# Attention on one core: the products with v put together behind the second step of side work, and the long product of a side step put first

## The chip, the core and the metric

The kernel runs on one core of one Trainium2 chip. The metric is the device time of one execution in microseconds (us). Within a core several engines run their own instruction streams, each in order, and wait for one another through semaphores: TensorE (PE in the profile; its weight loads are PEld), VectorE (DVE), ScalarE (ACT), GpSimd (POOL) and the queue that issues most transfers (SP).

## The reference

The reference is one transformer layer on 4 sequences of 512 tokens of width 512, in float32.

```python
x = x + cross_attention(layernorm(x), ctx)     # 16 heads of 32
x = x + moe(layernorm(x)) + shared_swiglu(layernorm(x))
```

In the cross attention, `q` comes from the tokens, `k` and `v` from a context of 512 rows of width 256. Queries and keys are normalized per head. The last 16 context rows have weights, keys and values of their own, and their attention is a second softmax whose result is added to that over the other 496 rows. The output is projected by `Wo`. Then a router picks 6 of 64 experts for each token, each expert takes at most 384 tokens and applies a gated feed-forward of width 352; a shared feed-forward of width 704 is added.

## The kernel before

The work has four stages in time: weights and the first context (up to about 110 us), the attention loop (to about 665 us) with the routing inside it, the shared feed-forward of the first sequences, and then the 64 experts with the combination at the end.

In the attention loop the 2048 tokens are 16 tiles of 128, and a tile is worked in four units, one for each group g of four heads. For a unit, `scores` (L351) multiplies queries and keys into two score tiles `ps`; `maximum` (L357, VectorE) takes row maxima `nm`; `exponentials` (L361, ScalarE) writes the probabilities `pr` and their sums; `mix_tail` (L368 and L369, VectorE) writes the 16 columns of the second softmax beside them. Then `turned` (L376) transposes each of the four slices of 128 keys into a bank `x`, `copied` (L381) copies it to `pT` (three by ScalarE, the fourth by VectorE), and `values` (L387) multiplies it with v into `pc`. The scores of the next unit are issued ahead of the transpositions of this one.

The loop that emits all this is written out by hand, and the order in which it is written is the order of the instructions on TensorE, ScalarE, VectorE and GpSimd. No planner changes it.

Into each unit two steps of side work are put by calls of `beside()`; there are thus eight numbered steps per tile, 0 to 7. Side work is a list of generators, each of which does one piece whenever it is asked:

- "query" (`query_tile`) prepares the queries of the tile after next: layer normalization on VectorE and GpSimd (`xn`, L313, then L314) at step 0, transposition of `xn` (L233) and copy `xnT` (L318) at step 2, the projection `mm` (L264) in two halves at steps 4 and 5, then `head_norm`: centring `hn_cen` (L242), square `hn_sq` (L244, GpSimd), and at step 0 of the next tile the variance (L248), a power on GpSimd (L251) and scaling (L252); at its step 3 the transposition into `qT`, at step 6 the scores of the 16 extra rows (L333 to L340).
- "context" (`context_tile`) prepares 128 rows of k and v for the next sequence: transposition at step 1, the k projection with its centring at step 2, the v projection (L305) with variance, power and scaling at step 3, the transposition of the keys at step 6. The fourth context tile of a sequence begins at step 5 of the tile before, so that its products are at steps 6 and 7. The last sequence has none to prepare, so tiles 12 to 15 run without.
- "finish" (`finish`) ends a tile: at step 7 it scales `pc`, at steps 0 and 1 come the two halves of the output projection with `wo`, the second layer normalization and `h` (L413, GpSimd), and in later tiles the transposition of h (step 4), the router (L433 to L443 at step 2, L456 to L459 at step 4, L462 to L473 at step 5) and six scatters of token numbers by GpSimd (L477, two each at steps 6, 7 and 0).

`owner` (L547) names for each of the eight steps the generator kind whose piece is a long projection there: finish at 0 and 1, context at 2 and 3, query at 4 and 5, none at 6 and 7. `beside()` sorts the list by whether a generator is of that kind; every generator of the kind is moved, also one of another tile that has no product at that step.

Three kinds of PSUM buffer matter: two banks `x`, taken in turn by all transpositions and small products, one bank `mm` for projections, and one bank `pc`. Whoever needs a bank again waits until its reader has emptied it.

Of the kernel before, what the change touches and what calls it, by code (L numbers as in the profile page):

```python
# [15 lines left out]
P = 128  # L16
B, S, D = 4, 512, 512
SC, KD = 512, 256
# [23 lines left out]
def xattn_moe_kernel(ctx, tc, a, out):  # L42
# [63 lines left out]
    def load_shared():  # L106
        for c in range(NC):
            sh_gu.append(slab(2 * FS))
            nc.sync.dma_start(sh_gu[-1], a["sh_guT"][c * P:(c + 1) * P, :])
        for f in range(0, len(FSC), 3):  # L110
            sh_down.append(slab(3, D))
            full = min(3, FS // P - f)
            nc.sync.dma_start(sh_down[-1][:, :full, :],
                              a["sh_downT"][f * P:(f + full) * P, :].rearrange("(c p) n -> p c n", p=P))
            if full < 3:
                nc.sync.dma_start(sh_down[-1][:FS % P, full, :], a["sh_downT"][(f + full) * P:, :])
# [39 lines left out]
    with ExitStack() as att:  # L156
# [188 lines left out]
        def scores(g, qT, kT):  # L345

            pss = []
            for r in range(NC):
                if r % 2 == 0:
                    pss.append(ps_s.tile([P, 2, SC], F32, tag="ps", name="ps"))  # L350
                nc.tensor.matmul(pss[-1][:, r % 2, :SM], qT[r * HD:(r + 1) * HD, g, :],  # L351
                                 kT[r * HD:(r + 1) * HD, g, :SM], start=True, stop=True)
            nm = small.tile([P, NC], F32, tag="nm", name="nm")
            return pss, nm

        def maximum(pss, nm, i):
            nc.vector.tensor_reduce(nm[:, 2 * i:2 * i + 2], pss[i][:, :, :SM], AX.X, ALU.max, negate=True)  # L357

        def exponentials(pr, pss, nm, sm, g, i):
            for r in (2 * i, 2 * i + 1):  # L360
                nc.scalar.activation(pr[:, r, :SM], pss[i][:, r % 2, :SM], AF.Exp, bias=nm[:, r:r + 1],  # L361
                                     accum_out=sm[:, g * NC + r:g * NC + r + 1])

        def mix_tail(pr, g, pd, rd, sm):

            hs = slice(g * NC, (g + 1) * NC)
            f = small.tile([P, NC], F32, tag="f", name="f")
            nc.vector.tensor_tensor(f, sm[:, hs], rd[:, hs], ALU.mult)  # L368
            nc.vector.tensor_tensor(pr[:, :, SM:], pd[:, hs, :], f.unsqueeze(2).to_broadcast([P, NC, DCA]),  # L369
                                    ALU.mult)  # L370
# [8 lines left out]
        def copied(tp, engine):  # L379
            pT = w2.tile([P, NC, P], F32, tag="pT", name="pT", bufs=5)  # L380
            (engine.copy if engine is nc.scalar else engine.tensor_copy)(pT, tp)  # L381
            return pT

        def values(pc, g, c, pT, kv):
            for r in range(NC):
                h = g * NC + r
                nc.tensor.matmul(pc[r * HD:(r + 1) * HD, g, :], kv[:, c, h * HD:(h + 1) * HD], pT[:, r, :],  # L387
                                 start=c == 0, stop=c == SC // P - 1)

        def inverse_sums(sm):  # L390

            rs = small.tile([P, H], F32, tag="rs", name="rs")
            nc.vector.reciprocal(rs, sm)
            wide = w2.tile([P, H, HD], F32, tag="wide", name="wide", bufs=1)
            nc.gpsimd.tensor_copy(wide, rs.unsqueeze(2).to_broadcast([P, H, HD]))
            return wide
# [114 lines left out]
        def new_context():  # L511
            return slab(NC, SC), slab(SC // P, D)
# [4 lines left out]
        def run(gens):  # L517

            left = []
            for g in gens:  # L520
                try:
                    next(g)
                    left.append(g)
                except StopIteration:
                    pass
            return left
# [5 lines left out]
        kvs, qTs, tail = {0: new_context()}, {}, {}  # L532
# [24 lines left out]
        for i in range(0, len(first), 2):  # L557
            side = first[i:i + 2]
            while side:
                side = run(side)  # L560
# [3 lines left out]
        side = []  # L564

        def beside():

            side.extend((n, make()) for n, make in begin.pop(step[0], ()))
            last = owner[step[0] % per_tile]
            for part in sorted(side, key=lambda p: p[0] == last):  # L570
                if next(part[1], side) is side:
                    side.remove(part)
            step[0] += 1

        def load_batch(b):
            for tn in range(b * TB, (b + 1) * TB):
                nc.sync.dma_start(acc[:, tn, :], a["x"][tn * P:(tn + 1) * P, :])
            load_y(b)
# [3 lines left out]
        with tc.manual_schedule(engines=engines):  # L582
            new = scores(0, qTs[0], kvs[0][0])
            pr = w2.tile([P, NC, SC], F32, tag="pr", name="pr")
            for i in range(2):
                maximum(*new, i)
                exponentials(pr, *new, tail[0][2], 0, i)
            for u, (t, g) in enumerate(units):
                b, i = divmod(t, TB)
                pd, rd, sm = tail[t]  # L590
                if g == 0:
                    pc = ps_c.tile([P, NC, P], F32, tag="pc", name="pc")
                    if i == 2 and b + 2 < B:
                        load_batch(b + 2)
                    if t == NT - 2:
                        load_shared()
                mix_tail(pr, g, pd, rd, sm)
                if g == NC - 1:
                    wide = inverse_sums(sm)
                pr_u = pr  # L600
                if u + 1 < len(units):
                    tn, gn = units[u + 1]
                    new = scores(gn, qTs[tn], kvs[tn // TB][0])
                    pr = w2.tile([P, NC, SC], F32, tag="pr", name="pr")
                pT = [copied(turned(pr_u, c), nc.scalar) for c in range(2)]
                if u + 1 < len(units):
                    maximum(*new, 0)
                    maximum(*new, 1)
                    exponentials(pr, *new, tail[tn][2], gn, 0)
                beside()  # L610
                pT.append(copied(turned(pr_u, 2), nc.scalar))
                pT.append(copied(turned(pr_u, 3), nc.vector))
                if u + 1 < len(units):
                    exponentials(pr, *new, tail[tn][2], gn, 1)
                for c in range(2):
                    values(pc, g, c, pT[c], kvs[b][1])
                if g < NC - 1:
                    beside()
                for c in range(2, SC // P):
                    values(pc, g, c, pT[c], kvs[b][1])  # L620
                if g == NC - 1:
                    side.append(("finish", finish(t, pc, wide)))
                    beside()

            class Here:
                hid = staticmethod(lambda: w2.tile([P, NC, SC], F32, tag="pr", name="pr")[:, :3, :])
                sg = staticmethod(lambda: w2.tile([P, NC, P], F32, tag="pT", name="pT", bufs=5).rearrange(
                    "p a b -> p (a b)"))
                pair = staticmethod(lambda: (lambda ps: (ps[:, 0, :], ps[:, 1, :]))(
                    ps_s.tile([P, 2, SC], F32, tag="ps", name="ps")))  # L630
                pd = staticmethod(lambda: ps_s.tile([P, 2, SC], F32, tag="ps", name="ps")[:, 0, :])

            def advance(steps, n):
                for _ in range(n):
                    next(steps, None)

            (_, oldest), (_, older), (_, newer) = side
            advance(oldest, 1)
            work = shared(0, Here)
            next(work)  # L640

            for n_older, n_newer in ((5, 2), (4, 0), (0, 3), (0, 2), (0, 4), (0, 2)):
                next(work)
                advance(older, n_older)
                advance(newer, n_newer)
                next(work)
            advance(newer, 4)
            lists_made = plan()
            for _ in range(TB):
                next(lists_made, None)  # L650
                next(work)
            for steps in (oldest, older, newer, lists_made, work):
                assert next(steps, None) is None
# [180 lines left out]
    with tc.manual_schedule(engines=engines):  # L834
# [64 lines left out]
        for i, b in enumerate(late):  # L899
            for n, _ in enumerate(others[b]):  # L900
# [8 lines left out]
                last = step == len(late) * slices  # L909
# [53 lines left out]
```

## Time and profile before

| | us |
|---|---|
| median of three runs | 1899.08 (1897.15 to 1904.79) |
| the profiled execution | 1896.93 |
| its span, from first to last instruction | 1895.1 |
| TensorE busy in the span | 1738.1 (92%) |
| VectorE, ScalarE, GpSimd busy | 852.3, 601.4, 677.7 |
| mean granted TensorE clock | 0.972 |

The profile is of one execution. Its lines name the engine, the line of the kernel, the operation, what it writes and reads by the program's names, and in brackets how long the engine stood idle before it and which instruction released it. A float32 product appears as two TensorE records. Times in the timeline are microseconds from the start of the span. The shares of busy time are means over stages with different limits, so a change inside the attention loop has to be read from that stretch. The granted clock is the share of full speed that TensorE was allowed.

### The profile page before, as it was taken

The page shows a single profiled execution, that of the slowest core. Times are in us where ns is not written, and L with a number is a line of the kernel's source. Part 1 is how long each engine was busy: PE and PEld are TensorE (multiplying, and loading weights), DVE is VectorE, ACT ScalarE, POOL GpSimd, SP SyncE. Part 2 cuts the span into 40 slices and gives each one's busy share as a digit, 9 for nine tenths or more (in the row PEclk, how much of TensorE's full clock was granted, in tenths as well). Part 3 has the DMA queues.
Part 4 walks back from the last instruction along what each step waited for, and adds up shares of the span by engine and source line. Part 5 has one row for each costly group of instructions (what it writes and reads, how often), then busy time and mean ns, then how long its engine had stood idle before and what let it go on. Part 6 is the DMA issues. An engine that isn't in the chain of part 4 may idle for free.

```text
span 1895.1 us, 28083 instructions
## 1 busy us (share of the span) xinstructions
PE 1738.1 (92%) x10556; PEld 1134.2 (60%) x10556; DVE 852.3 (45%) x1656; ACT 601.4 (32%) x1326; POOL 677.7 (36%) x620
## 2 busy tenths in 40 slices
PE   4689998999899898999999999999999999999994
PEld 1255555555555543476767767777777777666441
DVE  4256777777777732132322333333333333222565
ACT  0155565556566620022222222222232222222000
POOL 5435666655755332021211111221212122110776
PEclk9789999999999999999999999999999999999997
DMA  7000000010110114166876777787888787755676
GB/s 252 2 7 20 21 16 18 18 33 12 43 55 26 46 34 142 40 225 229 264 231 233 254 241 268 255 275 269 277 283 288 263 270 266 232 198 161 185 229 207
DMA packets 122658, 302.62 MB, mean 160 GB/s; under 512 B 16560, under 2 KB 44496, under 8 KB 114224
## 3 DMA queue, kind: packets, MB, share of 16 engines
q1 hardware_dynamic: 94928, 220.76, 34.2%
q0 software_dynamic: 26400, 76.16, 13.2%
q8 instruction: 197, 3.23, 0.7%
q10 hardware_dynamic: 1088, 2.10, 0.3%
q14 instruction: 45, 0.37, 0.1%
HBM read 235.28 MB, written 63.55 MB: 158 GB/s over the span
## 4 chain that ended last, share of the span: by engine, by line
PE 74%; DVE 10%; POOL 9%; DMA 3%; issue 3%; ACT 2%; SPq 0%; POOLq 0%; DVEq 0%
PE pg L743 16%; PE pd L782 10%; PE pu L743 10%; PE pd L788 6%; PE mm L264 5%; DVE nm L357 4%; PE x L376 3%; PE tx L731 3%; PE pu L764 3%; PE pg L128 3%; POOL hn_r L251 3%; PE pu L128 3%; PE pc L387 2%; PE pd L145 2%; PE x L233 2%
## 5 line engine op out<-in xcount | busy, mean ns | idle before, releaser
L690 POOL DMA_INDIRECT xg<-h_d,lists x192 | 182.0, 948 | 790.5 <-PE tx L731 716.1
L743 PE MATMUL pg<-xT,wgu 128*128 128x192 f32 (+4 forms) x1536 | 320.2, 351 | 11.2 <-issue 10.8
L743 PEld LDWEIGHTS pg<-xT,wgu 128*128 128x128 f32 x1536 | 257.8, 190 | 77.9 <-issue 57.9
L755 DVE TENSOR_TENSOR ehid<-sg,pu 128x384 f32<-128x384 f32 x128 | 70.9, 554 | 452.1 <-PE pu L743 446.7
L782 PE MATMUL pd<-wd,ehid 128*128 128x512 f32 (+1 forms) x408 | 213.2, 609 | 0.7 <-ACT eo L811 0.7
L743 PE MATMUL pu<-xT,wgu 128*128 128x192 f32 (+4 forms) x1024 | 205.9, 344 | 0.0
L754 ACT ACTIVATE sg<-pg 128x384 f32<-128x384 f32 x128 | 62.9, 491 | 380.2 <-PE pg L743 380.2
L743 PEld LDWEIGHTS pu<-xT,wgu 128*128 128x128 f32 x1024 | 176.0, 191 | 12.2 <-issue 1.5
L361 ACT ACTIVATE pr<-ps,nm 128x496 f32<-128x496 f32 x256 | 171.0, 677 | 17.3 <-DVE nm L357 16.4
L376 PEld LDWEIGHTS x<-ident,pr 128*128 128x128 f32 x1024 | 116.4, 145 | 92.7 <-issue 60.0
L381 ACT COPY pT<-x 128x512 f32<-128x512 f32 x192 | 106.6, 586 | 194.6 <-PE x L376 192.7
L376 PE MATMUL x<-ident,pr 128*128 128x128 f32 x1024 | 147.1, 286 | 14.8 <-DVE r_hot L458 8.3
L357 DVE TENSOR_REDUCE nm<-ps 128x2 f32<-128x992 f32 x128 | 145.2, 1173 | 17.2 <-PE ps L351 17.1
L788 PE MATMUL pd<-wd,ehid 128*64 128x256 f32 x1092 | 131.3, 384 | 9.0 <-ACT uh L771 4.4
L251 POOL TENSOR_TENSOR hn_r<-hn_var,mhalf 128x16 f32<-128x16 f32 (+1 forms) x33 | 96.6, 2927 | 95.6 <-DVE hn_var L249 80.7
L733 DVE COPY xT<-tx 128x512 f32<-128x512 f32 x192 | 126.0, 685 | 3.6 <-PE tx L731 2.1
L477 POOL DMA_INDIRECT list_d<-token_id,r_put x96 | 100.5, 1047 | 27.4 <-issue 24.9
L769 DVE TENSOR_TENSOR ehid<-sg,pg 32x384 f32<-32x384 f32 x64 | 35.8, 559 | 162.4 <-ACT sg L768 162.4
L788 PEld LDWEIGHTS pd<-wd,ehid 128*64 128x64 f32 x1092 | 78.1, 138 | 48.1 <-issue 7.4
L387 PE MATMUL pc<-pT,slab 128*32 128x128 f32 x2048 | 86.1, 289 | 3.4 <-DVE pT L381 2.7
L387 PEld LDWEIGHTS pc<-pT,slab 128*32 128x32 f32 x2048 | 50.5, 113 | 50.9 <-issue 39.9
L873 POOL DMA_INDIRECT g<-eo_d,slot_get x48 | 51.9, 1081 | 78.1 <-issue 66.7
(161 smaller groups left out, 2363.6 us busy)
## 6 DMA issues: line engine op xcount, KB each, us to landing
wgu<-in_w_gu SPq DMA_DIRECT2D x64, 1408.0 KB, 6.9
wd<-in_w_down SPq DMA_DIRECT2D x64, 512.0 KB, 6.6
eo_d<-eo SPq DMA_DIRECT2D x64, 512.0 KB, 5.2
eo_d<-eo SPq DMA_DIRECT2D x128, 128.0 KB, 4.8
wd<-in_w_down SPq DMA_DIRECT2D x64, 192.0 KB, 6.7
acc<-in_x SPq DMA_DIRECT2D x16, 256.0 KB, 5.2
h_d<-h SPq DMA_DIRECT2D x16, 256.0 KB, 2.0
h2T_d<-hT SPq DMA_DIRECT2D x16, 256.0 KB, 2.3
```

The source lines that it names most:

```text
L128: nc.tensor.matmul(dst, sh_gu[c][:, w0:w0 + P], xT[:, c, :], start=c == 0, stop=c == NC - 1)
L251: nc.gpsimd.tensor_tensor(r[:m], var[:m], mhalf[:m], ALU.pow)
L357: nc.vector.tensor_reduce(nm[:, 2 * i:2 * i + 2], pss[i][:, :, :SM], AX.X, ALU.max, negate=True)
L361: nc.scalar.activation(pr[:, r, :SM], pss[i][:, r % 2, :SM], AF.Exp, bias=nm[:, r:r + 1], accum_out=sm[:, g * NC + r:g * NC + r + 1])
L376: nc.tensor.transpose(tp[:, r, :], pr[:, r, c * P:(c + 1) * P], ident)
L381: (engine.copy if engine is nc.scalar else engine.tensor_copy)(pT, tp)
L387: nc.tensor.matmul(pc[r * HD:(r + 1) * HD, g, :], kv[:, c, h * HD:(h + 1) * HD], pT[:, r, :], start=c == 0, stop=c == SC // P - 1)
L690: nc.gpsimd.indirect_dma_start(out=x[:, :], out_offset=None, in_=h2_d[:, :], in_offset=bass.IndirectOffsetOnAxis(ap=lists[:, e * CT + c:e ...
L733: nc.vector.tensor_copy(xT[:, :, c * P:(c + 1) * P], tp)
L743: nc.tensor.matmul(dst[:, :n], wgu[:, c, w0:w0 + P], xT[:, c, :n], start=c == 0, stop=c == NC - 1)
L782: nc.tensor.matmul(pd, hid[:fn, fc, m * P:(m + 1) * P], wd[:fn, fc, :], start=fc == 0, stop=fc == len(FC) - 1)
L788: nc.tensor.matmul(pd[d * HALF:(d + 1) * HALF, i * D // 2:(i + 1) * D // 2], hid[:fn, fc, P + i * HALF:P + (i + 1) * HALF], wd[:fn, fc, d ...
```

## The change

Two edits in the attention loop. The key of the sort in `beside()` is inverted, so that at steps 0 to 5 the generators of the owner's kind come first and not last. And the products of the first two key slices with v no longer stand ahead of the second call of `beside()` of a unit: all four slices follow it. In the last unit of a tile, where the second call stands at the end, the order of the products stays as it was.

```diff
             side.extend((n, make()) for n, make in begin.pop(step[0], ()))
             last = owner[step[0] % per_tile]
-            for part in sorted(side, key=lambda p: p[0] == last):
+            for part in sorted(side, key=lambda p: p[0] != last):
                 if next(part[1], side) is side:
                     side.remove(part)
             step[0] += 1
...
                 if u + 1 < len(units):
                     exponentials(pr, *new, tail[tn][2], gn, 1)
-                for c in range(2):
-                    values(pc, g, c, pT[c], kvs[b][1])
                 if g < NC - 1:
                     beside()
-                for c in range(2, SC // P):
+                for c in range(SC // P):
                     values(pc, g, c, pT[c], kvs[b][1])
                 if g == NC - 1:
                     side.append(("finish", finish(t, pc, wide)))
```

Counted over the whole program, each engine has the same instructions as before. On TensorE, 16 v products follow one another where two groups of 8 had side work between them; on VectorE, the centring `hn_cen` (L242) now precedes the routing operations L433 to L443 at step 2 and L462 to L473 at step 5; on GpSimd, the two scatters of step 0 now precede the power, the scaling and `xn` of that step; on ScalarE, the key scaling (L258) precedes the copy `xnT` in three tiles; the order of SP's transfers is the same.

## The prediction

> **What bounds the kernel now.** I read the page first. TensorE is busy for 92% of the span, and the slices show where it is not full.
>
> ```profile
> PE 1738.1 (92%) x10556; PEld 1134.2 (60%) x10556; DVE 852.3 (45%) x1656; ACT 601.4 (32%) x1326; POOL 677.7 (36%) x620
> ```
>
> The change is confined to the attention loop (about 110 to 665 us). A table of stretches gives that stage's load; the columns are stretch, length, then busy us (and instructions) of PE, weight load, DVE, ACT, POOL, then clock, DMA share and GB/s.
>
> ```profile
> 150.00:650.00 500.00, 455.91 (x3986) 273.62 (x3988) 366.76 (x811) 294.88 (x729) 298.19 (x241) 0.98 0.08 26
> ```
>
> TensorE is full 91% of the time and the next engine, VectorE, 73%; DMA is 8%. At most 44 us of 500 are TensorE gaps, and only those can be won. The waits of TensorE from 109 to 612 us (total, times, longest) name them:
>
> ```profile
> PE x L233 <- POOL xn L313: 23.4, 13, 2.3
> PE x L376 <- DVE r_hot L458: 5.7, 6, 1.0
> PE x L233 <- DVE r_nm L426: 2.3, 8, 0.3
> ```
>
> The timeline of query tile 6 (its first scores start at 317.43) shows how each arises: start, length, engine, instruction, and in brackets the idle time before.
>
> ```profile
> 322.26 2.94 POOL L251 TENSOR_TENSOR hn_r<-hn_var,mhalf 128x16 f32<-128x16 f32 x1 [6.00 <-DVE hn_var L249]
> 326.95 2.08 POOL L313 TENSOR_SCALAR xn<-acc,ln_mv,ln_r 128x512 f32<-128x512 f32 x1
> 329.08 0.66 PE L233 MATMUL x<-ident,xn 128*128 128x128 f32 x4 [1.61 <-POOL xn L313]
> 329.57 1.88 PE L264 MATMUL mm<-slab,yT 128*128 128x512 f32 x4
> 341.38 0.53 DVE L458 TENSOR_TENSOR r_hot<-r_hot,x 128x384 f32<-128x384 f32 x1
> 341.97 1.09 PE L376 MATMUL x<-ident,pr 128*128 128x128 f32 x8 [0.95 <-DVE r_hot L458]
> 345.76 0.69 DVE L242 TENSOR_TENSOR hn_cen<-mm,bq 128x512 f32<-128x512 f32 x1 [0.32 <-PE mm L264]
> 346.53 1.04 POOL L244 TENSOR_TENSOR hn_sq<-hn_cen 128x512 f32<-128x512 f32 x1 [4.15 <-DVE f L368]
> 346.56 1.10 DVE L369 TENSOR_TENSOR pr<-pd,f 128x64 f32<-128x64 f32 x1
> 347.74 2.21 DVE L357 TENSOR_REDUCE nm<-ps 128x2 f32<-128x992 f32 x2
> 350.89 0.63 PE L233 MATMUL x<-ident,hn_sq 128*128 128x128 f32 x4 [0.28 <-DVE r_nm L426]
> ```
>
> To be seen: at step 2 of a tile TensorE waits 1.6 us for POOL's normalized rows and has a ready 1.88 us product right behind; at step 4 it waits 0.95 us for VectorE's L458; at step 6 it is released by VectorE, with no slack.
>
> [...]L369 takes 0.23 us alone, 1.10 us beside L244 (above). [...]after the 2.34 us waits of tiles 3 and 7 the granted clock read 0.50 in 222 to 224 and 372 to 374 us, after that of tile 11 it read 1.00; the 1.6 us waits left it at 1.00.
>
> **The change, part by part.** No instruction is added or removed. I count from tile 6's first scores (t = 0); tile numbers from 0.
>
> *Products with v (16 records, 0.64 us) move behind the second side step.* TensorE's sum is unchanged. What is lost is a cover: where the second side step starts with a transposition into an x bank and not with a product, that now follows the probabilities' transpositions at once and waits for ACT to empty a bank (copy 0.59, less the other 0.5 us of transpositions, plus hand-over: 0.3). This is step 3 of tiles 0, 3, 7, 11, 12, 13 and 14: 7 x 0.3 = **2 us lost**. The wait for the third and fourth pT copy does not grow: everything before it on TensorE stays.
>
> *Step 2, product first* (tiles 1, 2, 4, 5, 6, 8, 9, 10: those with a context product there). Before: free at 10.0, xn ready at 11.65. After: the product fills 10.0 to 11.9, then the xn transposition runs at once. But the product no longer covers xnT's copy: the transposition ends 12.5, ACT copies 12.6 to 13.2, and the second following transposition needs that bank; its predecessor ends 13.0, so some 0.4 to 0.45 us is paid back. 1.6 - 0.45 = 1.15; x 8 = **9.2 us won**. The product's VectorE reader hn_cen goes ahead of the routing work (max, index, hot, goes: 2.7 us), whose queue holds pT's fourth copy; that copy ends near 15.8, needed at 17.2, so hidden by the next product and v products; uncovered it would cost what it is late.
>
> *Step 4* (4, 5, 6, 8, 9, 10). The query product first removes the 0.24 us wait of L456 on pT, and in step 3 VectorE is earlier, since POOL's square no longer stands behind two scatters. L458 then comes 0.1 us after its bank's matmuls, 0.54 long, with 0.5 us of h transpositions as cover: 0.2 to 0.25 us of waiting stays. 0.95 + 0.24 - 0.25 = 0.94; I take 0.8, because hn_cen's place makes VectorE's line less free: 6 x 0.8 = **4.8 us won**.
>
> *Step 5, VectorE's queue* (tiles 2 to 13). Before, the eight routing operations L462 to L473 (1.6 us) ran while the product ran; after, hn_cen waits for the product's end E, and they follow it. hn_cen ends E + 0.75, L462 (0.54) E + 1.25, POOL's square runs E + 0.85 to 1.9; L464 [...]is held to 1.9; L464 to L473 take 1.06, f, the tail product and the reciprocal 0.45: the row maximum nm starts at E + 3.4. Before it started at E + 2.0 (347.74 - 345.72, the product's 343.84 + 1.88). The scores now follow at E + 1.15, as all 1.28 us of v products lie between, before at E + 0.5. So nm is 0.7 to 0.8 us later against TensorE, and step 6 has no slack: TensorE's transposition waits on VectorE (0.28 before). 12 x 0.8 = **9.6 us lost**. If L464 slips in before the square, 0.2; I take 0.8, since L462 outlasts the square's start.
>
> *Step 0, POOL's queue.* "finish" also owns the last two scatters of an older tile (L477, 2.4 to 2.7 us of POOL's time), so they jump ahead of the query's power, scaling, ln power and xn. In most tiles POOL idles 6.00 us there and they cost nothing. In tiles 3, 7 and 11 a second context tile's power and scaling end just then:
>
> ```profile
> 363.02 2.90 POOL L251 TENSOR_TENSOR hn_r<-hn_var,mhalf 128x16 f32<-128x16 f32 x1
> 369.80 0.66 PE L233 MATMUL x<-ident,xn 128*128 128x128 f32 x4 [2.34 <-POOL xn L313]
> 372.00:374.00 2.00, 2.00 (x21) 1.26 (x21) 1.43 (x3) 1.81 (x5) 1.67 (x3) 0.50 0.04 8
> ```
>
> The power moves from 363.0 to 365.5, xn from 369.75 to 372.25. The context's own transposition goes in front of it (0.5 us), and the last transposition of the step ends near 374.2, not 372.9: 3 x 1.3 = 3.9, plus a clock dip that tile 11 now also has (half clock over some 3.4 us: 1.7): **5.6 us lost**. The SP queue moves nothing: its order is the same, and h leaves POOL at the same place.
>
> Sum: -9.2 - 4.8 + 9.6 + 5.6 + 2 = +3.2 us. The page's execution took 1896.93 us (span 1895.1, 1.8 around it), 2.15 under the median of 1899.08; the difference carries over, as the expert stage starts on the attention's end and is TensorE's own. Forecast 1899.1 + 3.2 = 1902.3, say 1902: no change that can be told (0.5%, 9.5 us, is what a measurement tells from none).
>
> **Rivals.** *Faster*: VectorE's lateness at step 6 is not paid (place operations slip between) and the covers hold fully: 8 x 1.6 + 6 x 1.19 = 20 won, 7.6 lost: 12.4, 1887. For it: the largest single wait (23.4) has a ready product as cover. Against: the bank of xnT, and 350.89 shows no slack. *Slower*: in tiles 4 to 10 the routing's L440 ([...]at 13.4) meets POOL's h (L413, 2.08 us, at 13.7), which now starts earlier as no scatter is before it. [...]the fourth copy comes 0.6 us after need, nm at step 4 is 2 us later, and 4.8 + 6 x 0.9 is gone: 3.2 + 10.2 = 13.4: 1912.5. It decides within 0.3 us; L440 should be first. *It does nothing*: most of the waiting is set by chains that start at the scores and end at VectorE or POOL, and moving TensorE's work inside them leaves the end alone: 1899.
>
> **How the numbers follow.** Forecast 0.5, nothing 0.12, faster 0.17, slower 0.21. Within 0.5% is thus 0.62. The unknown terms (0.2 to 0.8 at step 6: 7 us; 1.3 to 3 in tiles 3, 7, 11: 5 us; gains of 0.4 less per tile: 5 us) carry the forecast from 1894 to 1910; with the rivals' nearer halves the range is 1888 to 1913.
>
> **What would show it.** Waits on xn near 0 in eight tiles, xnT's copy as a new 0.4 us wait there, above 3.5 us in tiles 3, 7 and 11; waits on r_hot under 0.3; the step 6 waits on r_nm near 1.1. Wrong if r_nm stays at 0.3 (then faster), or if pT's fourth copy (L381) on VectorE or r_hot appears among TensorE's long waits (then slower).

## The result: 0.7% slower, by a wait that no step of the prediction has

The changed kernel took 1917.75 us (median of five, 1913.80 to 1922.04) beside 1901.50 us for the kernel before (five, 1897.15 to 1904.79): ratio 1.0073, 95% interval 1.0049 to 1.0097. Forecast was 1902, range 1888 to 1913. The profiled execution took 1920.63 us (span 1918.9, mean clock 0.964).

The page's row of engines, and the same stretch of the attention loop as was shown of before:

```profile
PE 1743.0 (91%) x10556; PEld 1143.6 (60%) x10556; DVE 849.9 (44%) x1656; ACT 601.5 (31%) x1326; POOL 670.8 (35%) x620
```

```profile
150.00:650.00 500.00, 437.77 (x3830) 270.77 (x3830) 350.42 (x783) 284.07 (x700) 285.60 (x233) 0.96 0.08 26
```

The work in total is the same (10556 matmul records); in 500 us of the loop TensorE does 3830 of them where it did 3986. The loop loses most of the time: from the first transposition of `wide` (L233, at the end of tile 0) to the last (tile 15) it takes 551.0 us for 533.1, so 17.9 of the 23.8 us by which the span is longer; another 3.9 are lost behind it and 2.0 ahead of it. TensorE's waits of the changed kernel from 109 to 640 us (total, times, longest):

```profile
PE x L233 <- POOL xn L313: 21.0, 11, 4.2
PE x L376 <- ACT rb L402: 14.6, 9, 2.3
PE x L233 <- DVE r_nm L426: 5.0, 5, 1.1
PE x L376 <- DVE r_nm L426: 3.5, 3, 1.2
PE x L376 <- ACT xnT L318: 2.6, 11, 0.2
PE x L376 <- DVE r_hot L458: 2.5, 12, 0.2
```

Five of the six are in the prediction: xn (fewer, and longer in tiles 3, 7 and 11), r_nm at step 6 near 1.1, a small new wait on xnT, r_hot down to 0.2. The second is not: the transposition of the probabilities waits 14.6 us for `rb` (L402), ScalarE's copy of the transposed sums at the end of a tile. Before it did not appear.

The timeline of tile 6 of the changed kernel shows the predicted waits at about their sizes:

```profile
333.31 0.66 PE L233 MATMUL x<-ident,xn 128*128 128x128 f32 x4 [0.58 <-POOL xn L313]
346.17 0.69 DVE L242 TENSOR_TENSOR hn_cen<-mm,bq 128x512 f32<-128x512 f32 x1 [1.03 <-PE mm L264]
346.94 1.04 POOL L244 TENSOR_TENSOR hn_sq<-hn_cen 128x512 f32<-128x512 f32 x1 [3.30 <-DVE hn_cen L242]
347.35 0.65 DVE L464 SCALAR_TENSOR_TENSOR r_slot<-r_tf,r_place 128x6 f32<-128x6 f32 x1
349.41 2.22 DVE L357 TENSOR_REDUCE nm<-ps 128x2 f32<-128x992 f32 x2
352.56 1.08 PE L233 MATMUL x<-ident,hn_sq 128*128 128x128 f32 x4 [0.90 <-DVE r_nm L426]
```

The wait on xn fell from 1.61 to 0.58; L464 takes 0.65 us beside GpSimd's square and ends with it (348.00 and 347.98 us), where it took 0.17 before; the maxima are late, and step 6 waits 0.90 where it waited 0.28. So the forecast's sum was there, and something else came on top.

### The profile page after: what moved, and what is told of

It reads as the page before. It is cut to its first block, busy times and chain, and to the rows that moved or that the text cites. A ratio compares the mean times of both kernels' runs of the same rounds, so it can differ in the third digit from the quotient of the medians.

```text
span 1918.9 us, 28086 instructions
## 1 busy us (share of the span) xinstructions
PE 1743.0 (91%) x10556; PEld 1143.6 (60%) x10556; DVE 849.9 (44%) x1656; ACT 601.5 (31%) x1326; POOL 670.8 (35%) x620
## 4 chain that ended last, share of the span: by engine, by line
PE 71%; DVE 12%; POOL 9%; issue 3%; DMA 2%; ACT 2%; another core or an unknown queue 1%; SPq 0%; POOLq 0%; DVEq 0%; ACTq 0%
PE pg L741 15%; PE pd L780 10%; PE pu L741 10%; PE pd L786 6%; DVE nm L357 5%; PE mm L264 4%; PE x L376 3%; POOL hn_r L251 3%; PE pg L128 3%; PE tx L729 3%; PE pu L762 3%; PE pd L145 3%; PE pu L128 2%; PE ps L128 2%; PE pc L387 2%
## 5 line engine op out<-in xcount | busy, mean ns | idle before, releaser
L376 PE MATMUL x<-ident,pr 128*128 128x128 f32 x1024 | 153.1, 288 | 33.3 <-ACT rb L402 15.7
L786 PE MATMUL pd<-wd,ehid 128*64 128x256 f32 (+1 forms) x1092 | 130.4, 380 | 9.9 <-issue 6.3
L786 PEld LDWEIGHTS pd<-wd,ehid 128*64 128x64 f32 (+1 forms) x1092 | 78.3, 137 | 47.8 <-issue 9.1
L477 POOL DMA_INDIRECT list_d<-token_id,r_put x96 | 95.6, 996 | 28.6 <-issue 26.2
L264 PE MATMUL mm<-slab,yT 128*128 128x512 f32 x128 | 72.5, 695 | 9.2 <-DVE hn_cen L242 7.8
L351 PE MATMUL ps<-slab,qT 32*128 32x496 f32 x512 | 78.0, 636 | 3.0 <-ACT pr L361 2.7
L387 PE MATMUL pc<-pT,slab 128*32 128x128 f32 x2048 | 77.1, 287 | 2.0 <-DVE pT L381 1.3
```

The costliest lines, as they stand in the source:

```text
L264: nc.tensor.matmul(ps[:m], lT[:, c, :], w[:, c, :], start=c == 0, stop=c == n - 1)
L376: nc.tensor.transpose(tp[:, r, :], pr[:, r, c * P:(c + 1) * P], ident)
L786: nc.tensor.matmul(pd[d * HALF:(d + 1) * HALF, i * D // 2:(i + 1) * D // 2], hid[:fn, fc, P + i * HALF:P + (i + 1) * HALF], wd[:fn, fc, d ...
```

## Where rb is late, and a difference in the records themselves

At the end of a tile TensorE transposes `wide` (L233) and ScalarE copies the bank to `rb`. The end of tile 8 in the changed kernel; start, length, engine, instruction:

```profile
433.83 0.97 POOL L477 DMA_INDIRECT list_d<-token_id,r_put  x1 [0.30 <-issue]
435.10 0.97 POOL L477 DMA_INDIRECT list_d<-token_id,r_put  x1 [0.30 <-issue]
436.37 0.97 POOL L477 DMA_INDIRECT list_d<-token_id,r_put  x1 [0.30 <-issue]
...
435.37 0.66 PE L233 MATMUL x<-ident,wide 128*128 128x128 f32 x4
...
439.19 0.66 PE L376 MATMUL x<-ident,pr 128*128 128x128 f32 x4 [1.53 <-ACT rb L402]
...
438.56 0.58 ACT L402 COPY rb<-x 128x512 f32<-128x512 f32 x1 [3.17 <-PE x L376]
```

The transposition is over at 436.03, ScalarE is free from 435.4, and rb waits for nothing but TensorE's semaphore; yet it starts 2.5 us after the end of the transposition. In the trace, TensorE's four semaphore updates due from 436.0 to 437.7 all appear between 438.53 and 438.71, 0.06 us apart, right behind the last landing (438.52) of the sixth scatter, L477. The change put the two scatters of step 0 directly behind the four of steps 6 and 7: six in a row. The scatter's line ends at 437.34, 1.18 us before that; the last recorded landings of these scatters come 1.0 to 1.2 us after their lines' ends.

The same trace is also not complete: it holds 1505 of TensorE's semaphore events where that of before holds 1635, and of the 16 landings of a scatter inside a row often 3 to 5. I call such a record *gapped* and the other *full*. The 20 traces of this study are one or the other, with nothing between (1486 to 1506 events, or 1635), and kernels run at one time on one chip shared the kind; one chip had both. All kinds of run are labelled so below. In each of the three groups with gapped records the changed kernel stood first, in the others not; whether that matters was not tried.

## The experiments

### One part of the change at a time: full records

Four kernels at one time. *scatters_first* is the kernel before with one thing changed, *scatters_last* the changed kernel with that thing undone: the place of the older "finish" at steps 0 and 1, whose only work there is the two scatters.

```diff
-            for part in sorted(side, key=lambda p: p[0] == last):        # scatters_first
+            newest = [p for p in side if p[0] == "finish"][-1:]
+            old = lambda p: p[0] == "finish" and p not in newest and last == "finish"
+            for part in sorted(side, key=lambda p: -1 if old(p) else p[0] == last):
...
+            for part in sorted(side, key=lambda p: 2 if old(p) else p[0] != last):   # scatters_last
```

> The kernel before with one thing changed: at step 0 of a tile the two scatters of an older finish come first in the side work, as in the changed kernel; TensorE's, VectorE's and ScalarE's orders stay as before. Theory (the six scatters in a row make the copy rb late, and hold the query's chain in tiles 3, 7 and 11): some ten waits of 1 to 2.3 us on rb appear, the xn waits of tiles 3, 7 and 11 go from 2.3 to about 5 us; 12 to 20 us slower than before. Rival (rb is late because VectorE is late from step 5 on, or because of TensorE's new order): no waits on rb, only the three xn waits grow; 4 to 9 us slower.

> The changed kernel with one thing undone: at step 0 the older finish generators, with their two scatters, come last again. Theory: the waits on rb vanish and the xn waits of tiles 3, 7 and 11 fall from 4.2 to near 0.5 to 2.3 us; 16 to 22 us faster than the changed kernel, thus 0 to 5 us faster than before. Rival: the waits on rb stay at 10 to 15 us, and it is 10 us or more slower than before.

*centre_last* is the changed kernel with the centring `hn_cen` of steps 2 and 5 emitted after the routing's operations; *both_undone* has this and the scatters last. A generator yields `"more"` behind its product, and is called on when the others have had their turn:

```diff
+            yield "more"                     # behind the product, in query_tile and context_tile
...
-                if next(part[1], side) is side:
+                said = next(part[1], side)
+                if said is side:
                     side.remove(part)
+                elif said == "more":
+                    more.append(part)
+            for part in more:
+                next(part[1])
```

> The changed kernel with one thing undone: at steps 2 and 5 the product still comes first on TensorE, but its centring comes behind the routing operations on VectorE again. Theory (the step 5 order costs 0.7 to 0.8 us in tiles 2 to 13 and some clock): the waits on r_nm at step 6 fall from 1 us to 0.3, and it is 8 to 12 us faster than the changed kernel, still 4 to 8 us slower than before. Rival (rb's lateness comes from VectorE): the waits on rb vanish too, 20 us faster than the changed kernel.

> The changed kernel with both undone: scatters last at step 0 and the centring behind the routing; what is left is the long product first on TensorE and the v products together. Theory: the xn waits of the eight tiles with a product are absorbed (1.1 us each), the r_hot waits fall to 0.2 us, step 6 waits stay at 0.3: 8 to 14 us faster than before. Rival (the waits at the steps are set by VectorE and POOL, whatever TensorE does): within 4 us of before.

Measured against the kernel before (1892.19 us at that time): scatters_first 1.0021 (1.0008 to 1.0035), scatters_last 1.0035 (1.0014 to 1.0056), centre_last 1.0014 (0.9989 to 1.0040), both_undone 0.9962 (0.9949 to 0.9976). None had a wait on rb. The longest waits of scatters_first from 109 to 640 us and, of *both_undone* (whose lines are numbered one or two further), from 109 to 660; ahead of them that on r_hot of before, from 109 to 660:

```profile
PE x L376 <- DVE r_hot L458: 8.3, 8, 1.3
```

```profile
PE x L233 <- POOL xn L313: 31.4, 13, 5.0
```

```profile
PE x L378 <- DVE r_hot L460: 11.9, 14, 1.4
PE x L233 <- POOL xn L314: 10.4, 11, 2.1
PE mm L264 <- DVE hn_cen L242: 10.0, 7, 1.4
```

Two of the prediction's mechanisms are isolated here. Scatters first lengthen the waits on xn (23.4 to 31.4, the longest now 5.0): tiles 3, 7 and 11 are 3.9, 2.4 and 4.7 us longer. They also take most of the waiting on r_hot away (8.3 to 1.8 from 109 to 660 us), and each of the tiles 4 to 6 and 8 to 10 is 1.17 us shorter. And undoing the centring trades the waits on r_nm (3.1 us left in both_undone) for 10.0 us on `mm`, whose reader is now late.

With the scatters last, the centring first is expensive by another path. The chain in tile 5 of *scatters_last*:

```profile
293.09 0.98 POOL L477 DMA_INDIRECT list_d<-token_id,r_put  x1 [0.30 <-issue]
296.84 1.03 POOL L244 TENSOR_TENSOR hn_sq<-hn_cen 128x512 f32<-128x512 f32 x1
297.90 0.69 DVE L248 TENSOR_REDUCE hn_var<-hn_sq 128x16 f32<-128x512 f32 x1 [3.56 <-POOL hn_sq L244]
302.21 0.53 DVE L458 TENSOR_TENSOR r_hot<-r_hot,x 128x384 f32<-128x384 f32 x1
302.80 0.44 PE L376 MATMUL x<-ident,pr 128*128 128x128 f32 x2 [3.12 <-DVE r_hot L458]
```

The two scatters delay GpSimd's square, VectorE stands 3.56 us in front of the variance that reads it, and the maxima, the routing and r_hot follow: 3.12 us of waiting at step 4. With the scatters first the same r_hot costs 0.20. So the gain of step 4 needs the scatters out of the way, and the two parts are not additive.

### The change and its parts again: gapped records

Four kernels at another time (before: 1905.27 us). *sort_only* has the inverted key and the v products divided as before; *values_only* the v products together and the old key; *best_split* the inverted key, the v products divided as before, the query's centring behind the routing at step 5 only, and the older scatters last in tiles 3, 7 and 11 alone.

```diff
-            for part in sorted(side, key=lambda p: p[0] == last):     # sort_only
+            for part in sorted(side, key=lambda p: p[0] != last):
```

```diff
-                for c in range(2):                                    # values_only
-                    values(pc, g, c, pT[c], kvs[b][1])
                 if g < NC - 1:
                     beside()
-                for c in range(2, SC // P):
+                for c in range(SC // P):
```

> The changed kernel once more. Its first profile shows 15.7 us of waits on the copy rb, always until the last of six scatters in a row has landed, and many semaphore records missing at these places; two kernels with the same six scatters in a row (scatters_first, centre_last) show neither. Theory (those waits belong to that execution's recording, not to the kernel): no waits on rb, nothing missing; the rest as before: xn near 18 us, r_nm 7 to 12 us, r_hot near 5; 0.2 to 0.6% slower than before. Rival (they belong to this order of the instructions): the waits on rb come back with 10 us or more, and it is 0.7% slower or worse.

> The kernel before with only the sort inverted: the v products of the first two slices stay ahead of the second step. Theory (the loss comes from the sort; moving the v products costs 2 us at the steps 3 that have no product): 0 to 3 us faster than the changed kernel, waits of TensorE transpositions on pT (0.8 to 1.4 us in seven places) gone, r_nm as in the changed kernel. Rival (a good part of the loss is the v products' move): no slower than before, and over 5 us faster than the changed kernel.

> The kernel before with only the v products of all four slices put behind the second step; the sort as before, so that transpositions come ahead of the long product there and wait for a bank x. Theory: new waits of L233 on pT, 0.3 to 0.7 us at the second steps of the first three units of nearly every tile; 5 to 15 us slower than before. Rival (the bank is free in time): within 3 us of before.

> Built from what the runs showed: long product first; v products where they were before; centring ahead of the routing at step 2 but behind it at step 5; the two scatters first at step 0 except in tiles 3, 7 and 11, where they come last. Theory: waits on xn below 12 us, r_hot below 5, r_nm at 2 to 4, hn_cen none, pT near 2; half-clock time at most that of before; 14 to 24 us faster than before. Rival (a shorter wait at one step is paid at the next, as the chain of VectorE or POOL sets the pace): no better than both_undone, 4 to 10 us faster.

The changed kernel gave 1.0094 (1.0064 to 1.0125), sort_only 1.0175 (1.0143 to 1.0208), values_only 1.0001 (0.9985 to 1.0017), best_split 1.0103 (1.0039 to 1.0167). best_split, which was to be the best of all, was slower than the kernel before. The waits on rb were back in the three kernels with six scatters in a row (10.2, 6.9 and 3.3 us from 100 to 680 us), and all but absent in values_only (0.3). The sum of these waits does not rank the losses. In best_split rb starts 3.3 to 4.2 us after `wide` does in ten tiles, and the loss shows more in TensorE's busy time than in its waits: the scores alone are busy for 83.3 us from the first `wide` to the last (L352), before for 65.8 (L351). The clock has a share in that, at half for 41.0 us of this stretch, before for 20.5 (a product at half clock took 3.14 us for 1.88 in the changed kernel). At that point it looked like a matter of which parts stand together.

values_only settles one term. The waits on pT from 109 to 640 us, before and in values_only, and the v products in one tile (the groups by line, 279.69 to 316.85 us of before and 282.26 to 319.08 us of values_only; busy us and mean ns stand behind the bar):

```profile
PE x L233 <- ACT pT L381: 1.8, 4, 0.8
```

```profile
PE x L233 <- ACT pT L381: 9.2, 24, 1.6
```

```profile
L387 PE MATMUL pc<-pT,slab 128*32 128x128 f32 x132 | 5.4, 279 | 0.0
```

```profile
L387 PE MATMUL pc<-pT,slab 128*32 128x128 f32 x132 | 4.8, 276 | 0.0
```

The wait on pT grows from 1.8 us to 9.2, in 24 places, not 7; but 16 products in one run keep TensorE 0.6 us less per tile than two groups of 8. Over the tiles the two cancel.

### The same four at one time: which kind of record decides

To separate "this order of the kernel" from "this kind of time", the changed kernel ran beside three variants that had shown no wait on rb.

> The changed kernel again, beside three of its variants on one chip at one time. Two theories for the waits of the exponentials' transposition on rb (L376 on L402, 14.6 us in 9 waits in the profile after). K, the kernel's order: they come with step 2's product first, the centring ahead of the routing and six scatters in a row together, so they are here again (9 to 11 waits, 10 to 15 us), and the three variants, which showed none the first time, show none again. S, the state of the chip: at some times the records of the scatters' landings are incomplete (3 to 5 of 16 for each) and TensorE's semaphore updates come through only with the last landing of a row of scatters; then here rb is late only if it is such a time, and every kernel with six scatters in a row shares it. K and S: ratio 1.007 to 1.012 where the waits are there; S without them: about 1.000.

> The kernel before with the older finish's two scatters first at step 0, so six in a row, and nothing else changed. K: no wait on rb and 1.002 as the first time. S: where the changed kernel beside it has waits on rb, so has this one (8 to 11 waits of 1.1 to 1.9 us), its landings' records are incomplete too, and its ratio is 1.007 to 1.012 in place of 1.002; where the changed kernel has none, this one is 1.002.

> The changed kernel with these two scatters last again, so four in a row whose last landing comes before rb is due. K and S both: no wait on rb. Ratio 1.0035 as before under K; under S as well, since nothing waits for rb. If it is well above that (1.007 or more) without a wait on rb, a third cause is at work.

> The changed kernel with the scatters last and the centring behind the routing at steps 2 and 5: product first at the other steps and the v products together are all that is left. K and S: no wait on rb, ratio 0.995 to 0.998, below 1 again at another time.

All four records were gapped, and *scatters_first*, the same kernel as above, now had this from 109 to 640 us:

```profile
PE x L233 <- POOL xn L313: 31.2, 13, 5.0
PE x L376 <- ACT rb L402: 9.6, 6, 2.4
```

Its ratio was 1.0162 (1.0110 to 1.0215) in place of 1.0021. The waits on xn are the same to 0.2 us; those on rb are new. The changed kernel gave 1.0082 (1.0058 to 1.0106), scatters_last 1.0023 (1.0006 to 1.0039), both_undone 0.9965 (0.9950 to 0.9979). So the kernel's order alone (K) is refuted, and the theory of the time (S) gave the right signs for all four; it expected 1.012 at most for scatters_first, and that was 4 thousandths short. Beside each other at this time, the changed kernel and scatters_last differ in the place of the two scatters alone: 1.0082 and 1.0023, with intervals that do not meet. With full records the same difference went the other way: scatters_last was at 1.0035 and the changed kernel, in the next section, at 0.9989, each against the kernel before at its own time.

### Full records again: what the change is worth without the wait

*row_cut* is the changed kernel with the row of six broken: before the two scatters of step 0 GpSimd copies a column of this tile's rb, so that they start after it.

```diff
+            latest[0] = rb                   # in finish, behind the copy to rb
...
+                if k == 4:
+                    cut = small.tile([P, 1], F32, tag="cut", name="cut")
+                    nc.gpsimd.tensor_copy(cut, latest[0][:, 0, :1])
                 nc.gpsimd.indirect_dma_start(
...
-            for part in sorted(side, key=lambda p: p[0] != last):
+            newest = [p for p in side if p[0] == "finish"][-1:] if last == "finish" else []
+            for part in sorted(side, key=lambda p: -1 if p in newest else p[0] != last):
```

> The kernel before, for its profile beside the others at one time. If the chip is in the state with incomplete landings: no wait on rb, since its four scatters in a row have landed before rb is due (0.6 us after the wide transposition starts, rb at 0.69), and a span of 1895 to 1908 us. Ratio 1.000 by construction.

> The changed kernel. With incomplete landings: 8 to 11 waits on rb, ratio 1.007 to 1.011. With complete landings: no wait on rb, and the ratio falls to 0.998 to 1.005, since the waits on rb are 10 to 15 us of its 15 us loss in the other state[...].

> The changed kernel in which GpSimd, ahead of the two scatters of step 0, copies one column of this tile's rb into a scrap tile, so that the row of six is cut into four and two and the two start after rb. Length of the row is the cause: no wait on rb, no other wait in its place, 9 to 14 us faster than the changed kernel beside it, ratio about 1.000 to 1.003. Any scatter under way holds TensorE's semaphore updates back: rb is on time, but the copies of pT and the maxima that wait for TensorE next come 1 to 3 us late in the same ten tiles, and the ratio stays at 1.006 or above. Special tiles have xn at most 1 us later.

> The changed kernel with the centring behind the routing at steps 2 and 5, scatters six in a row as in the changed kernel. With incomplete landings: 8 to 11 waits on rb as in the changed kernel (there were none with complete ones), ratio 1.008 to 1.014 in place of 1.0014. With complete landings: none, 1.0014.

These records were full. The kernel before had no wait on rb (span 1896.6); the changed kernel gave 0.9989 (0.9972 to 1.0006), centre_last 1.0002 (0.9983 to 1.0020), row_cut 0.9962 (0.9945 to 0.9979). The changed kernel's waits from 109 to 660 us, and the end of tile 8:

```profile
PE x L233 <- POOL xn L313: 17.7, 11, 4.2
PE x L233 <- DVE r_nm L426: 6.9, 7, 1.1
PE x L376 <- DVE r_nm L426: 5.7, 5, 1.2
PE x L376 <- DVE r_hot L458: 4.1, 14, 1.3
```

```profile
421.55 0.97 POOL L477 DMA_INDIRECT list_d<-token_id,r_put  x1 [0.30 <-issue]
422.83 0.97 POOL L477 DMA_INDIRECT list_d<-token_id,r_put  x1 [0.30 <-issue]
...
421.83 0.66 PE L233 MATMUL x<-ident,wide 128*128 128x128 f32 x4
...
422.52 0.58 ACT L402 COPY rb<-x 128x512 f32<-128x512 f32 x1 [0.68 <-PE x L233]
```

The program, its order and the scatters' times against `wide` are those of the gapped profile above; rb starts 0.69 us after the start of the transposition instead of 3.19. What that does to a tile is seen in tile 5, from one `wide` to the next, in the first profile of the changed kernel and here:

```profile
281.41:319.52 38.11, 34.18 (x294) 21.13 (x290) 27.25 (x62) 21.72 (x54) 23.99 (x20) 0.96 0.06 19
```

```profile
278.25:312.93 34.68, 32.60 (x294) 20.09 (x291) 27.01 (x62) 21.68 (x54) 23.29 (x20) 1.00 0.07 20
```

3.43 us more with the same 294 records: TensorE waits 1.6 on rb, 1.0 on `pd`, which is late behind it, and 0.4 more on xn, and is spared the 1.0 on r_nm; and it is busy 1.6 us longer, the clock reading 0.96 against 1.00. Before, the tile took 37.16.

*row_cut* was run twice more for its question, whether the row's length is the cause.

> The same kernel as row_cut, in the hope of a time with incomplete landings (3 to 5 of 16 recorded for the scatters inside a row). If so, and the length of the row is the cause: no wait on rb, no other new wait over 1 us in its place, ratio 0.996 to 1.003, where the changed kernel had 1.007 to 1.009. If any scatter under way holds TensorE's semaphore updates back: rb is on time, the copies of pT or the maxima next to it come 1 to 3 us late in ten tiles, ratio 1.006 or above. If all landings are recorded: no wait on rb and 0.996 as before, which decides nothing.

> The same kernel as row_cut once more. With incomplete landings, length of the row as the cause: no wait on rb, no other new wait over 1 us, ratio 0.996 to 1.003; any scatter under way as the cause: other waits of 1 to 3 us in ten tiles and 1.006 or above. With all landings recorded: 0.996 to 0.998, and the question stays open.

Both records were full: 0.9975 (0.9954 to 0.9996) and 0.9943 (0.9923 to 0.9962). It beats the kernel before three times of three, but it never ran at a gapped time, so its question is undecided by it.

### Reading the row's length from the runs at hand

Within one gapped run the tiles differ in when their row of scatters ends, and the traces answer a part. In tile 14 the row has six scatters in every kernel but *row_cut*, the kernel before among them. Times are us from the start of the `wide` transposition to the start of the row's last scatter and to the start of rb; tiles 3 to 14.

| kernel, record | tiles | scatters in the row | last scatter | rb |
|---|---|---|---|---|
| any but row_cut, full | 3 to 5, 7 to 9, 11 to 14 | 4 or 6 | -2.5 to 1.9 | 0.69 or 0.70; once 1.15, at the half clock |
| values_only, gapped | 4, 5, 8, 9 | 4 | -1.6 | 0.69 |
| values_only, gapped | 3, 7, 11, 12, 13 | 4 | -0.7 | 1.28 to 1.37 |
| values_only, gapped | 14 | 6 | 1.6 | 4.01 |
| changed, gapped | 5 | 6 | 0.1 | 2.24 |
| changed, gapped | 4, 8, 9 | 6 | 1.0 | 3.18 to 3.24 |
| changed, gapped | 12 | 6 | 0.8 | 3.00 |
| changed, gapped | 14 | 6 | 1.6 | 3.85 |
| changed, gapped | 3, 7, 11, 13 | 6 | 1.8 or 1.9 | 3.98 to 4.07 |
| both, gapped | 6, 10 | 2 and 2, or 1 and 2, apart | -0.4 | 0.64 |

With gapped records rb starts 1.9 to 2.4 us after the start of the row's last scatter whenever that is later than 0.69; this holds for four in a row as for six, and in the other gapped kernels too. Two in a row, which start at -1.8 and -0.4 and whose last recorded landings in the changed kernel's first trace are at 1.7 and later, delay nothing: rb starts at 0.64. Four last too short a time to cost: in values_only, rb 0.6 us late makes TensorE wait for 0.3 us in all. So the change did not make the delay, which is there in values_only as well; it made the row reach 1.7 to 2.6 us further into the next tile. The last tile is an exception: in tile 15 of the first profile the row goes on to 4.0 and lands at 8.2, but rb starts at 3.15, and in six more of the nine gapped traces it starts over 3 us before the last landing as well. What ends the delay is thus not known for every row. That two separate scatters behind rb would be harmless, as *row_cut* has them, follows from the last row of the table, but was only argued.

## Why the prediction was wrong

**The step that failed is "Step 0, POOL's queue".** It said of the scatters that jump ahead: "In most tiles POOL idles 6.00 us there and they cost nothing." As a statement on GpSimd's time it held. But the two scatters join the four of steps 6 and 7, and in the first profile TensorE's semaphore updates came through only at about the time when the last one landed (in tile 8 the first of four at 438.53 us, the landing at 438.52). Ten of the tiles 3 to 14 have such a row, and between 109 and 690 us TensorE waited 15.7 us in the first profile for rb, 10.2 and 13.0 in the next two, plus what follows behind. With the scatters put last at the same gapped time, the ratio was 1.0023 for 1.0082. Between the first profile and the full one the stretch from the first `wide` to the last is 28.5 us longer (551.0 against 522.6): TensorE waits 67.1 us for 47.4 and is busy 482.6 for 474.7. Not all of this belongs to the row of six, since a gapped time makes the same stretch 8.2 us longer in scatters_last and 4.8 in both_undone. The prediction had nothing for it. I asked of each moved scatter what is queued behind it on its engine, and not what else is under way when it lands. The profile of before could not have warned of this: its record is full, and in its tile 14, with six scatters in a row, rb starts at 0.69.

Point by point, against the full record, where the forecast's terms can be seen alone:

- **Step 2** (1.15 a tile): in tile 5 the wait on xn goes from 1.6 to 0.2 and a wait on xnT of 0.2 appears: 1.2. Right. In the gapped record 0.57 of xn stayed.
- **Step 4** (0.8 a tile): r_hot 1.0 to 0.2, and L456's 0.2 gone: 1.0. Right in size, and in its reason, that the square no longer stands behind two scatters; *scatters_first* and *scatters_last* show that without this the wait is 3.1.
- **Step 5** (0.8 lost a tile): r_nm in tile 5 from 0.3 to 1.0; in all 3.9 us of waits became 12.6, 8.7 lost for the 9.6 forecast. Right. L464 ended with the square, as the step says; its 0.65 us stands above, and before it took 0.17.
- **Step 0, tiles 3, 7 and 11** (5.6 lost): xn waits 4.2, and these tiles are 2.4, 1.7 and 3.4 us longer, 7.5 in all. Right in mechanism, some low.
- **Products with v** (2 lost): mis-sized, in both parts. The waits on pT were 7.4 us more in *values_only*, not 2, and the packing won 0.6 us a tile that the prediction had as "TensorE's sum is unchanged". Net nothing measurable.

So for the full record the sum of +3.2 us stands against a ratio of 0.9989, -2 us (-5 to +1). That is inside the range, but not by the forecast's terms. In the profiled pair of that time the stretch from the first `wide` to the last takes 522.6 us for 532.9: TensorE waits 1.8 us less and is busy 8.6 us less. The largest missing term is the packing: the v products (L387) are busy 77.3 us in all where before had 85.1. Against it stands the clock, at half for 34.1 us of this stretch; before had 20.5 and 17.1 in its two profiles, and the prediction counted one stretch more. The clock was lower in every execution (0.960 to 0.969 over the whole span; before 0.970 to 0.977), but what that costs was not separated, and one kernel, centre_last, had 44.4 and 20.5 us in its two full records. The terms do not add up to the medians either: the profiled executions are 9.4 us apart, the medians 2.0. Where the rest lies is open.

The rivals: the slower one, L440 meeting h, did not happen (L440 took 0.56 us in every tile, and r_hot stays at 0.2). That h would keep L440 to its own end was not shown either: the one L440 of before that ran beside h, at 619.70 us, took 0.94 us for 0.56 and ended 0.91 us ahead of h. Slower it was, but by none of them.

## What to carry to other kernels

When a DMA is moved within its queue, look at what it now stands next to, and at every semaphore that other engines post while it lands; here six scatters, the last of which starts up to 1.9 us behind the transposition of `wide`, cost time at gapped times where four did not (1.0082 against 1.0023). Measure the same pair of kernels at more than one time before a few tenths of a per cent are explained, and look at whether the traces are complete: here the change was worth -0.1% or +0.7 to +0.9% with the same program. If an order is wanted that does not depend on this, keep the product first and leave the scatters last and the centring behind the routing: *both_undone* gave 0.9962 with full and 0.9965 with gapped records.

## What the runs showed of the hardware

- **Semaphore updates behind a row of scatters.** Four TensorE updates due over 1.7 us came 0.06 us apart behind the last landing. Why only at gapped times is open. Missing records and late updates occur in the same gapped runs; that the two have to do with each other is not shown. All five times of the changed kernel carry the slowdown (1913.80 to 1922.04, the profiled one 1920.63); whether the recording has a part in it cannot be told from them.
- **The kernel before was slower at those times as well:** 1905.27 and 1903.62 us where the records of its neighbours were gapped, 1890.78 to 1893.27 where they were full. It was not itself profiled at a gapped time, so where these 10 to 15 us lie was not seen. A part is likely to lie behind the attention loop: from the last `wide` to the end every gapped trace takes 1231.1 to 1235.2 us, and every full one 1222.3 to 1228.8, whatever the kernel.
- **The half clock behind a wait.** In the first profile the wait of 0.90 us at step 6 of tile 6 (shown above, at 352.56) is followed by a product of 3.14 us where 1.88 is usual, and the granted clock read 0.51 from 352.5 to 356.0 us and 1.00 in the next microsecond:

```profile
353.44 3.14 PE L264 MATMUL mm<-slab,yT 128*128 128x512 f32 x4
```

The 1.0 us on r_nm in tile 5 of the full record left the clock at 1.00. The dip that the prediction counts in tile 11 was there: in the changed kernel's first profile the clock read 0.50 over 6.8 us in each of tiles 3, 7 and 11 (from 219.4, 373.0 and 526.6), beginning within waits on xn of 4.2 us. In the profile of before it read 0.51 over 3.5 us in tiles 3 and 7 (from 221.4 and 371.6), beginning 0.6 and 1.8 us behind the end of waits of 2.34. What decides whether the half clock follows a wait was not shown.
